# The last graph layer of a four-layer graph network: two heads side by side in TensorE's columns

## The chip, the cores and the metric

The kernel runs on one core of a Trainium2 chip. The metric is the device time of one execution in microseconds (us); lower is better. The engines of the core are named as in the profile: PE is TensorE (PEld its weight loads), DVE is VectorE, ACT is ScalarE, POOL is GpSimd, and SP issues transfers.

## The reference

The network takes 3125 nodes of 256 values and 100,000 edges through four layers. Each layer adds a graph layer and a mixer to the nodes, and then a feed-forward part. The change lies in the graph layer of the last one, a graph attention with four heads of 64 values:

```python
xp = (x @ W).reshape(n, N_HEADS, HEAD_DIM)
a_src = jnp.einsum('nhc,hc->nh', xp, att_src)
a_dst = jnp.einsum('nhc,hc->nh', xp, att_dst)
e = jax.nn.leaky_relu(a_src[src] + a_dst[dst], NEG_SLOPE)
e_max = jax.ops.segment_max(e, dst, num_segments=n)
e_exp = jnp.exp(e - e_max[dst])
denom = jax.ops.segment_sum(e_exp, dst, num_segments=n)
alpha = e_exp / denom[dst]
out = jax.ops.segment_sum(alpha[:, :, None] * xp[src], dst, num_segments=n)
```

So every target node gets, in each head, a weighted mean of the values of its source nodes. The result goes through relu and is added to x, together with the mixer of that layer (`_L3_mix_ref`, a linear attention with two layer norms and a small two-layer net). The last feed-forward part (one expert of eight per node) comes after both.

## The kernel before

**Layout.** Nodes stand in 25 blocks of 125 (`P = 125`, `NB = 25`). Targets are walked in pieces of 500 columns (`PW = 500`, `PIECES`: six of 500 and one of 125), two pieces at a time, so there are three groups of 1000 targets and a last one of 125.

**The dense form.** Nothing is gathered in this layer. An earlier stage has counted, for each pair of a source and a target, the edges between them and a loop per node, in bfloat16 (`ctt_d`). The weight of a pair is exp of a leaky relu of a sum, and this is the larger of two products of a source factor and a target factor. A factor that only the target has cancels in the division, so with r = exp(0.8 a_dst + bias), u0 = exp(a_src - top) and u1 = exp(0.2 (a_src - top)), the weight is max(r u0, u1). It is made for 125 sources and 1000 targets of a head in two instructions: ACT computes t = relu(r u0 - u1) (line 1899), DVE computes z = (t + u1) x counts (line 1902).

**Aggregation.** TensorE then multiplies z by the source values (line 1905). The stationary operand is `xr[:, b, k4, :]`, 125 sources by 65 columns: the 64 values of the head and a column of ones, which gives the sum of the weights. The moving operand is z, 500 targets at a time, and everything is float32. The result of a head and a piece, 65 x 500, adds up over the 25 source blocks in one PSUM bank; two heads and two pieces take the four banks `acc0` to `acc3`. In the loops, a group of targets (`p0`) holds two pairs of heads (`h0`), which hold 25 source blocks (`b`), which hold two heads (`h`) of two pieces (`k`). The last group takes all four heads at once, 125 targets of each. The counts of a block come through the SP queue into `cs`, which has three buffers, in two transfers, of 112 and of 13 rows (`move`, lines 134 and 135).

**Target factors.** At the start of each group, r is needed for all heads and targets, the same on all 125 partitions. Lines 1875 to 1881 make it on TensorE: the column of weights that gives a_dst is repeated 125 times as stationary operand and multiplied by the transposed nodes, two matmuls for each head and piece (line 1878), and ACT takes exp of the result (line 1880).

**End of a pair of heads.** The four banks are copied to SBUF by DVE and ACT in turn (`evac`, lines 141 and 143), TensorE turns them block by block (line 1920), and `finish` divides by the sum of weights, takes relu and adds to x, with five small DVE instructions for each block and pair of heads (lines 1860 to 1867). A sum below 1e-20 is noted in `few`; a note there would send the program into another, general path at the end.

**The order of work.** `l3_gnn_mix` runs the dense part and the mixer `l3_mix_by_pieces` together: `together` always advances the one whose reported progress is less, with the mixer's counted down by 1.15. All engines work down one fixed list, which the tile framework sets when the program is built. When both have finished a piece of nodes, `arrive` sends that piece on to the norm and the routing of the last feed-forward part.

Of the kernel before, what the change touches and what calls it, by code (L numbers as in the profile page):

```python
# [12 lines left out]
F32 = mybir.dt.float32  # L13
# [4 lines left out]
AF = mybir.ActivationFunctionType  # L18
OP = mybir.AluOpType
# [4 lines left out]
N = 3125  # L24
D = 256
P = 125
NB = 25
HB = D // 128
# [9 lines left out]
PW = 500  # L38
# [47 lines left out]
PIECES = [(i, min(PW, N - i)) for i in range(0, N, PW)]  # L86


class Net:
# [1692 lines left out]
    def l3_gnn_mix(self, before, arrivals):  # L1782
# [5 lines left out]
        nc, a = self.nc, self.a  # L1788
        with ExitStack() as s:
            ms = s.enter_context(self.pool("m3_sb"))  # L1790
            with self.pool("m3_w") as sb:
                w = self.load_w(sb, "L3_gnn_W")
                wx = self.attn_cols(sb, w, "wx", ["L3_gnn_att_src", "L3_gnn_att_dst"], ms)
            mix = self.l3_mix_by_pieces(ms, None)
# [4 lines left out]
            sb = s.enter_context(self.pool("g3_sb"))  # L1799
            wk = s.enter_context(self.pool("g3_wk", 2))  # L1800
            pa = s.enter_context(self.pool("g3_ps", 1, space=PSUM))
            xr = sb.tile([P, NB, 4, 65], F32, name="xr")
            nc.gpsimd.memset(xr[:, :, :, 64:65], 1.0)
            al = sb.tile([P, NB, 8], F32, name="al")
            for b in range(NB):
                ps = self.bank()
                self.mm_tok(ps[:P, :264], self.xt, b, wx)
                nc.vector.tensor_copy(xr[:, b, :, :64], ps[:P, :D].rearrange("p (h d) -> p h d", h=4))
# [9 lines left out]
            ps = self.bank()  # L1818
# [4 lines left out]
            bias = sb.tile([P, 4], F32, name="bias3")  # L1823
# [14 lines left out]
            self.together([self.l3_dense(sb, wk, pa, wx, xr, us, bias), mix], (1.0, 1.15))  # L1838

    def together(self, parts, pace=(1.0, 1.0)):  # L1840

# [5 lines left out]
            except StopIteration:  # L1847
                del at[p]

    def l3_dense(self, sb, wk, pa, wx, xr, us, bias):  # L1850
# [5 lines left out]
        at = free[:65, 8 * PW:12 * PW].rearrange("p (h d) -> p h d", h=2)  # L1856

        def finish(b, h0, nh, acc):

            nc.vector.tensor_scalar(few[:, b, h0:h0 + nh], acc[:, :, 64], 1e-20, None, op0=OP.is_lt)  # L1860
            rd = wk.tile([P, 4], F32, name="rd")
            nc.vector.tensor_scalar(rd[:, :nh], acc[:, :, 64], 1e-20, None, op0=OP.max)
            nc.vector.reciprocal(rd[:, :nh], rd[:, :nh])
            t = wk.tile([P, 4, 64], F32, name="tf")
            nc.vector.tensor_mul(t[:, :nh], acc[:, :, :64], rd[:, :nh, None].to_broadcast([P, nh, 64]))
            v = self.x[:, b, h0 * 64:(h0 + nh) * 64]
            nc.vector.scalar_tensor_tensor(v, t[:, :nh].rearrange("p h d -> p (h d)"), 0.0, v,
                                           op0=OP.max, op1=OP.add)

        done, there = 0, []  # L1870
        for p0 in range(0, len(PIECES), 2):
            pcs = PIECES[p0:p0 + 2]
            n = sum(w for _, w in pcs)
            for h in range(4):
                for k, (i, w) in enumerate(pcs):
                    ps = self.bank()
                    for c in range(HB):
                        nc.tensor.matmul(ps[:P, :w], wx[:, c, 260 + h:261 + h].to_broadcast([128, P]),
                                         self.xt[:, c, i:i + w], start=(c == 0), stop=(c == HB - 1))
                    nc.scalar.activation(rows[:, h, k * PW:k * PW + w], ps[:P, :w], AF.Exp, bias=bias[:, h:h + 1],  # L1880
                                         scale=0.8)
            hg = 4 if n < PW else 2
            for h0 in range(0, 4, hg):
                acc = {}
                for h in range(hg):
                    for k in range(len(pcs)):
                        acc[h, k] = pa.tile([65, 512], F32, name=f"acc{h * len(pcs) + k}")
                for b in range(NB):
                    cs = wk.tile([P, 2, PW], BF, name="cs", bufs=3)
                    if len(pcs) == 2:  # L1890
                        self.move(nc.sync, cs, self.ctt_d[p0:p0 + 2, :, b, :].rearrange("k p d -> p k d"))
                        c = cs.rearrange("p k d -> p (k d)")
                    else:
                        self.move(nc.sync, cs[:, 0, :n], self.ctt_d[p0, :, b, :n])
                        c = cs[:, 0, :n]
                    for h in range(hg):
                        k4 = h0 + h
                        t = wk.tile([P, 2 * PW], F32, name="t5")
                        nc.scalar.activation(t[:, :n], rows[:, k4, :n], AF.Relu, bias=us[:, 2, b, k4:k4 + 1],  # L1899
                                             scale=us[:, 0, b, k4:k4 + 1])  # L1900
                        z = wk.tile([P, 2 * PW], F32, name="z", bufs=3)
                        nc.vector.scalar_tensor_tensor(z[:, :n], t[:, :n], us[:, 1, b, k4:k4 + 1], c,  # L1902
                                                       op0=OP.add, op1=OP.mult)
                        for k, (i, w) in enumerate(pcs):
                            nc.tensor.matmul(acc[h, k][:, :w], xr[:, b, k4, :], z[:, k * PW:k * PW + w],  # L1905
                                             start=(b == 0), stop=(b == NB - 1))
                        done += n
# [5 lines left out]
                if hg == 2:  # L1913
                    for h in range(2):
                        for k, (i, w) in enumerate(pcs):
                            self.evac(at[:, h, k * PW:k * PW + w], acc[h, k][:, :w])
                    for j in range(n // P):
                        ps = self.bank()
                        for h in range(2):
                            nc.tensor.transpose(ps[:P, h * 65:(h + 1) * 65], at[:, h, j * P:(j + 1) * P],  # L1920
                                                self.ident[:65, :65])
                        finish(p0 * 4 + j, h0, 2, ps[:P, :130].rearrange("p (h c) -> p h c", h=2))
                        yield done / (NB * N * 4)
                else:
                    for h in range(4):
                        self.evac(at[:, h // 2, h % 2 * P:(h % 2 + 1) * P], acc[h, 0][:, :P])
                    ps = self.bank()
                    for h in range(4):
                        nc.tensor.transpose(ps[:P, h * 65:(h + 1) * 65], at[:, h // 2, h % 2 * P:(h % 2 + 1) * P],
                                            self.ident[:65, :65])  # L1930
                    finish(p0 * 4, 0, 4, ps[:P, :260].rearrange("p (h c) -> p h c", h=4))
# [426 lines left out]
```

## Time and profile before

| what | value |
|---|---|
| time, median of 7 runs | 4972.23 us (4964.39 to 4976.81) |
| profiled execution | 4981.08 us, span 4979.2 us |
| mean granted clock of TensorE over the span | 0.842 |
| dense stage of the last graph layer | 3801 to 4709 us, 908 us |
| TensorE, DVE, ACT busy in it | 878.4, 604.8, 534.5 us |
| aggregation (line 1905) | 1400 records, first at 3809.9, last at 4708.1 us |

A matmul of float32 stands in the trace as two records, each with its own weight load. A record's time on PE overlaps that of the next one, so the distance between starts tells what one costs. In a group of instructions, "128\*125 128x500" means 128 rows and 125 columns of stationary operand, and a moving operand of 500 columns.

### The profile page before, as it was taken

The numbers are of one execution on the slowest core, as the hardware profiler recorded it, in microseconds if no ns is written. First come the engines' busy times: TensorE is split into PE (matmuls) and PEld (weight loads), VectorE is DVE, ScalarE is ACT, GpSimd is POOL, SyncE is SP. The second block draws the span as 40 slices with busy tenths as digits, with TensorE's granted clock in tenths as the row PEclk, the third lists the DMA queues.
The fourth block names the chain that finished last, engine by engine and source line by source line (L and its number), as shares of the span: only waits on it lengthen the run. The fifth ranks groups of instructions, "written<-read, shape, count | busy, mean of one in ns | idle before, by whom it ended". The sixth has DMA issues, their size and how long they took to land. (4 is left out here: it accounts for less than half of the span.)

```text
span 4979.2 us, 49604 instructions
## 1 busy us (share of the span) xinstructions
PE 3795.7 (76%) x16425; PEld 2469.0 (50%) x16425; DVE 2466.1 (50%) x7872; ACT 1322.6 (27%) x2364; POOL 1125.2 (23%) x1124
## 2 busy tenths in 40 slices
PE   1886995899477799995555555455499999999798
PEld 0675993566345465554343333334265444444465
DVE  6885344544656311144343434445345666667644
ACT  1475100111132233331000000000045655455611
POOL 1000004000440100004666666666000000000011
PEclk8785995899787799997767677767699999999799
DMA  6244512433230000003333333333301112111142
GB/s 177 61 138 122 127 33 54 135 115 119 72 71 5 24 13 13 13 6 89 92 92 95 89 95 93 88 83 91 123 1 29 49 47 59 39 50 49 40 135 68
DMA packets 256291, 360.32 MB, mean 72 GB/s; under 512 B 62959, under 2 KB 199097, under 8 KB 256028
## 3 DMA queue, kind: packets, MB, share of 16 engines
q1 hardware_dynamic: 132514, 168.96, 11.7%
q0 software_dynamic: 66480, 135.56, 10.1%
q10 hardware_dynamic: 57033, 52.54, 3.8%
q8 instruction: 135, 2.21, 0.2%
q14 instruction: 129, 1.05, 0.1%
HBM read 270.31 MB, written 94.92 MB: 73 GB/s over the span
## 5 line engine op out<-in xcount | busy, mean ns | idle before, releaser
L1564 PE MATMUL acc<-hg,to 128*125 128x256 f32 x1682 | 584.5, 497 | 559.2 <-DVE to L1562 193.6
L1551 POOL DMA_INDIRECT hg<-hx_d,idx x841 | 827.4, 984 | 434.8 <-issue 241.4
L1564 PEld LDWEIGHTS acc<-hg,to 128*125 128x125 f32 x1682 | 382.3, 243 | 748.0 <-DVE to L1562 234.0
L1905 PE MATMUL acc<-z,xr 125*65 125x500 f32 (+1 forms) x1400 | 576.1, 554 | 10.4 <-DVE z L1902 8.5
L1902 DVE SCALAR_TENSOR_TENSOR z<-t,us,cs 125x1000 f32<-125x1000 f32 (+1 forms) x400 | 410.1, 1029 | 139.8 <-PE acc L1905 103.7
L1899 ACT ACTIVATE t<-xn,us 125x1000 f32<-125x1000 f32 (+1 forms) x400 | 409.6, 1037 | 237.4 <-DVE z L1902 232.3
L1905 PEld LDWEIGHTS acc<-z,xr 125*65 125x65 f32 x1400 | 188.4, 144 | 314.2 <-issue 272.5
L1562 DVE SCALAR_TENSOR_TENSOR to<-lock,keep,to 128x125 f32<-128x125 f32 x841 | 258.2, 345 | 169.0 <-remote 82.8
L1560 DVE TENSOR_SCALAR to<-iota_f,rel_b,wgt 128x125 f32<-128x125 f32 x841 | 269.2, 359 | 75.7 <-remote 46.2
L1422 DVE SCALAR_TENSOR_TENSOR x<-ps,lg,x 125x256 f32<-125x256 f32 x200 | 94.1, 483 | 415.4 <-PE ps L233 415.4
L239 PE MATMUL ps<-xt,w 128*128 128x500 f32 (+1 forms) x672 | 267.7, 545 | 1.8 <-DMA w<-in_L_ffn_W_dram 1.8
L2188 POOL DMA_INDIRECT bx_d<-row,slot x25 | 31.4, 1256 | 929.9 <-ACT t L1899 812.1
L779 ACT ACTIVATE k<-k 125x128 f32<-125x128 f32 x50 | 15.8, 317 | 801.5 <-DVE to L1562 322.5
L571 PE MATMUL ps<-y,cb 125*125 125x256 bf16 x1875 | 215.8, 280 | 0.0
L571 PEld LDWEIGHTS <-cb 125*125 125x125 bf16 x1875 | 214.5, 141 | 0.2
L168 ACT ACTIVATE rstd_t<-rstd_t 125x4 f32<-125x4 f32 (+2 forms) x86 | 17.3, 204 | 663.0 <-DVE rstd_t L167 420.1
L233 PE MATMUL ps<-wo,h 128*125 128x256 f32 x800 | 187.7, 386 | 3.6 <-ACT h L1416 2.6
L239 PE MATMUL ps<-h,w 128*128 128x500 f32 (+1 forms) x448 | 180.7, 546 | 7.8 <-ACT h L1411 7.8
L239 PEld LDWEIGHTS ps<-xt,w 128*128 128x128 f32 x672 | 122.4, 192 | 113.7 <-issue 108.1
L239 PE MATMUL pl<-xbt,w 128*128 128x384 f32 x416 | 172.2, 563 | 8.2 <-DVE xbt L1135 5.8
L233 PEld LDWEIGHTS ps<-wo,h 128*125 128x125 f32 x800 | 142.9, 187 | 65.8 <-ACT h L1416 43.7
L452 PE MATMUL t<-ky,lo 128*128 128x75 bf16 (+4 forms) x1251 | 138.7, 253 | 37.5 <-ACT ct L455 22.3
(558 smaller groups left out, 6179.4 us busy)
## 6 DMA issues: line engine op xcount, KB each, us to landing
cs<-ctt_d SPq DMA_DIRECT2D x150, 218.8 KB
w<-in_L_ffn_w_dram SPq DMA_DIRECT2D x52, 512.0 KB
cnt_d<-cd SPq DMA_DIRECT2D x25, 683.6 KB
cb<-cnt_d SPq DMA_DIRECT2D x25, 683.6 KB
ctt_d<-ct ACTq DMA_DIRECT2D x6, 2734.4 KB
hg<-hx_d,idx POOLq DMA_INDIRECT x841
b0x_d<-zero SPq DMA_DIRECT2D x1, 9984.0 KB
xb<-b0x_d SPq DMA_DIRECT2D x26, 384.0 KB
```

Source lines behind the costliest of these rows:

```text
L233: self.nc.tensor.matmul(ps, xt[:, h, b * P:(b + 1) * P], w[:, h, :], start=(h == 0), stop=(h == k - 1))
L239: self.nc.tensor.matmul(ps, w[:, h, :], xt[:, h, i:i + n], start=(h == 0), stop=(h == k - 1))
L452: nc.tensor.matmul(t[:, w * 25 * r:(w + 1) * 25 * r], lo[:, :, n % 4], ky[:, :25 * r, n % 4], start=(j == 0), stop=(j == ws[w0 + w][2] - 1))
L571: nc.tensor.matmul(ps[:P, :D], cf[k][:, h * P:(h + 1) * P], y3[:, b0 + k, j, :], start=(k == 0 and j == 0), stop=(k == m - 1 and j == 2))
L1422: nc.vector.scalar_tensor_tensor(self.x[:, b, :], ps[:P, :D], g[:, b, e:e + 1], self.x[:, b, :], op0=OP.mult, op1=OP.add)
L1551: nc.gpsimd.indirect_dma_start(out=hg[:, j, :], out_offset=None, in_=hx, in_offset=bass.IndirectOffsetOnAxis(ap=idx[:, c + j:c + j + 1], a ...
L1560: nc.vector.tensor_scalar(to, self.iota_f[:, :P], rel[:, c + j:c + j + 1], wgt[:, c + j:c + j + 1], op0=OP.is_equal, op1=OP.mult)
L1562: nc.vector.scalar_tensor_tensor(to, lock[:, b, :], keep[:, j:j + 1], to, op0=OP.max, op1=OP.mult)
L1564: nc.tensor.matmul(ps, to, hg[:, j, :D], start=(c + j == c0[b]), stop=(c + j == c0[b + 1] - 1))
L1899: nc.scalar.activation(t[:, :n], rows[:, k4, :n], AF.Relu, bias=us[:, 2, b, k4:k4 + 1], scale=us[:, 0, b, k4:k4 + 1])
L1902: nc.vector.scalar_tensor_tensor(z[:, :n], t[:, :n], us[:, 1, b, k4:k4 + 1], c, op0=OP.add, op1=OP.mult)
L1905: nc.tensor.matmul(acc[h, k][:, :w], xr[:, b, k4, :], z[:, k * PW:k * PW + w], start=(b == 0), stop=(b == NB - 1))
```

## The change

The heads of a pair share the columns of TensorE. The value matmul has 64 stationary columns instead of 65; the first head of the pair goes to columns 0 to 63, the second to 64 to 127 (`tile_position=(0, 64 * j)`), and both write one bank of 128 rows. The sums of weights are separate matmuls: 32 columns of ones, in tiles at columns 0, 32, 64 and 96 of a third bank, one for each head and piece. A half group uses three banks, and they rotate over four (`turn`).

The target factors are computed once for all nodes, before the loop: exp of `al` on ACT, one transpose on TensorE, a copy by DVE, a store to DRAM (`r_d`). `target_rows` loads them spread over the 125 partitions, through the SP queue, one load of 4 KB per partition for each head and group (again in parts of 112 and 13 rows), at the end of the half group that used those rows last.

`finish` copies three banks instead of four, turns the sums in one bank and the values in another for four blocks at once, and uses wider DVE instructions. The t tiles lie in a spare part of `xn`, z has four buffers instead of three, and TensorE's instructions of a block come after the z of all its heads.

```diff
-            xr = sb.tile([P, NB, 4, 65], F32, name="xr")
-            nc.gpsimd.memset(xr[:, :, :, 64:65], 1.0)
+            xr = sb.tile([P, NB, 4, 64], F32, name="xr")
...
+            r = sb.tile([P, 4, NB], F32, name="r3")
+            for h in range(4):
+                nc.scalar.activation(r[:, h], al[:, :, 4 + h], AF.Exp, bias=bias[:, h:h + 1], scale=0.8)
+            ps = self.bank()
+            nc.tensor.transpose(ps[:4 * NB, :P], r.rearrange("p h b -> p (h b)"), self.ident[:P, :P])
+            rt = sb.tile([4 * NB, P], F32, name="rt3")
+            nc.vector.tensor_copy(rt, ps[:4 * NB, :P])
+            r_d = self.dram.tile([4, N], F32, name="r3_d")
+            nc.sync.dma_start(r_d.rearrange("h (b p) -> (h b) p", p=P), rt)
...
+        def target_rows(g, h0):
+
+            if g < len(groups):
+                i, n = groups[g][0][0], sum(w for _, w in groups[g])
+                for h in (h0, h0 + 1):
+                    self.move(nc.sync, rows[:P, h, :n], r_d[h, i:i + n].partition_broadcast(P))
+
+        def finish(b, nb, h0, nh, acc):
+
+            w, nu = nb * P, len(acc) - 1
+            at = wk.tile([128, 3, PW], F32, name="at", bufs=1)
+            for k in range(nu + 1):
+                self.evac(at[:, k, :w], acc[k][:, :w])
+            ps = self.bank()
+            for j in range(nb):
+                nc.tensor.transpose(ps[:P, j * 128:(j + 1) * 128], at[:, nu, j * P:(j + 1) * P], self.ident)
...
-            for h in range(4):
-                for k, (i, w) in enumerate(pcs):
-                    ps = self.bank()
-                    for c in range(HB):
-                        nc.tensor.matmul(ps[:P, :w], wx[:, c, 260 + h:261 + h].to_broadcast([128, P]),
-                                         self.xt[:, c, i:i + w], start=(c == 0), stop=(c == HB - 1))
-                    nc.scalar.activation(rows[:, h, k * PW:k * PW + w], ps[:P, :w], AF.Exp, bias=bias[:, h:h + 1],
-                                         scale=0.8)
...
+            for hs in ((0, 2),) if len(pcs) == 1 else ((0,), (2,)):
+                units = [(h0, k, w) for h0 in hs for k, (_, w) in enumerate(pcs)]
+                acc = [pa.tile([128, 512], F32, name=f"acc{(turn + j) % 4}") for j in range(3)]
+                turn += 3
...
-                        for k, (i, w) in enumerate(pcs):
-                            nc.tensor.matmul(acc[h, k][:, :w], xr[:, b, k4, :], z[:, k * PW:k * PW + w],
-                                             start=(b == 0), stop=(b == NB - 1))
...
+                    for u, (h0, k, w) in enumerate(units):
+                        for j in range(2):
+                            nc.tensor.matmul(acc[u][64 * j:64 * j + 64, :w], xr[:, b, h0 + j, :],
+                                             zs[h0 + j][:, k * PW:k * PW + w], start=(b == 0), stop=(b == NB - 1),
+                                             tile_position=(0, 64 * j))
+                    for u, (h0, k, w) in enumerate(units):
+                        for j in range(2):
+                            q = 32 * (2 * u + j)
+                            nc.tensor.matmul(acc[2][q:q + 32, :w], self.ones[:P, :32],
+                                             zs[h0 + j][:, k * PW:k * PW + w], start=(b == 0), stop=(b == NB - 1),
+                                             tile_position=(0, q))
...
+                for h0 in hs:
+                    target_rows(g + 1, h0)
+                finish(b0, pcs[0][1] // P, hs[0], 2 * len(hs), acc)
```

More of the change, by code (lines that the diff above doesn't have):

```diff
@@ L1807, in l3_gnn_mix @@
                 self.mm_tok(ps[:P, :264], self.xt, b, wx)
-                nc.vector.tensor_copy(xr[:, b, :, :64], ps[:P, :D].rearrange("p (h d) -> p h d", h=4))
+                nc.vector.tensor_copy(xr[:, b], ps[:P, :D].rearrange("p (h d) -> p h d", h=4))
                 nc.scalar.copy(al[:, b, :], ps[:P, 256:264])
@@ L1837, in l3_gnn_mix @@
             mix.send(mw)
-            self.together([self.l3_dense(sb, wk, pa, wx, xr, us, bias), mix], (1.0, 1.15))
+            self.together([self.l3_dense(sb, wk, pa, xr, us, r_d), mix], (1.0, 1.15))
     def together(self, parts, pace=(1.0, 1.0)):
@@ L1848, in together, with l3_dense @@
                 del at[p]
-    def l3_dense(self, sb, wk, pa, wx, xr, us, bias):
+    def l3_dense(self, sb, wk, pa, xr, us, r_d):
         nc = self.nc
@@ L1855, in l3_dense @@
         rows = free[:, :8 * PW].rearrange("p (h d) -> p h d", h=4)
[L1856 to L1868, printed above, removed]
@@ L1870, in l3_dense @@
-        done, there = 0, []
-        for p0 in range(0, len(PIECES), 2):
-            pcs = PIECES[p0:p0 + 2]
-            n = sum(w for _, w in pcs)
-            for h in range(4):
-                for k, (i, w) in enumerate(pcs):
-                    ps = self.bank()
-                    for c in range(HB):
-                        nc.tensor.matmul(ps[:P, :w], wx[:, c, 260 + h:261 + h].to_broadcast([128, P]),
-                                         self.xt[:, c, i:i + w], start=(c == 0), stop=(c == HB - 1))
-                    nc.scalar.activation(rows[:, h, k * PW:k * PW + w], ps[:P, :w], AF.Exp, bias=bias[:, h:h + 1],
-                                         scale=0.8)
[L1882 to L1887, printed above, removed]
+        spare = [free[:P, j * PW:(j + 2) * PW] for j in (8, 10)]
@@ new lines, in l3_dense @@
+        groups = [PIECES[p:p + 2] for p in range(0, len(PIECES), 2)]
+        def target_rows(g, h0):
[11 more added lines that the diff above has]
+                nc.tensor.transpose(ps[:P, j * 128:(j + 1) * 128], at[:, nu, j * P:(j + 1) * P], self.ident)
+            sums = ps[:P, :nb * 128].rearrange("p (j q r) -> p j q r", j=nb, r=32)[:, :, :, 0]
+            rd = wk.tile([P, 4, 4], F32, name="rd")
+            f = wk.tile([P, 4, 4], F32, name="fw")
+            nc.vector.tensor_scalar(f[:, :nb], sums, 1e-20, None, op0=OP.is_lt)
+            nc.vector.tensor_scalar(rd[:, :nb], sums, 1e-20, None, op0=OP.max)
+            nc.vector.reciprocal(rd[:, :nb], rd[:, :nb])
+            for k in range(nu):
+                bk, hk = (b + 4 * k, h0) if nh == 2 else (b, 2 * k)
+                nc.vector.tensor_copy(few[:, bk:bk + nb, hk:hk + 2], f[:, :nb, 2 * k:2 * k + 2])
+                ps = self.bank()
+                for j in range(nb):
+                    nc.tensor.transpose(ps[:P, j * 128:(j + 1) * 128], at[:, k, j * P:(j + 1) * P], self.ident)
+                t = wk.tile([P, 4, 2, 64], F32, name="tf")
+                nc.vector.tensor_mul(t[:, :nb], ps[:P, :nb * 128].rearrange("p (j h d) -> p j h d", j=nb, d=64),
+                                     rd[:, :nb, 2 * k:2 * k + 2, None].to_broadcast([P, nb, 2, 64]))
+                v = self.x[:, bk:bk + nb, hk * 64:hk * 64 + 128]
+                nc.vector.scalar_tensor_tensor(v, t[:, :nb].rearrange("p j h d -> p j (h d)"), 0.0, v,
+                                               op0=OP.max, op1=OP.add)
@@ L1888, in l3_dense @@
+        done, there, turn = 0, [], 0
+        for h0 in (0, 2):
+            target_rows(0, h0)
+        for g, pcs in enumerate(groups):
+            b0 = pcs[0][0] // P
+            n = sum(w for _, w in pcs)
+            for hs in ((0, 2),) if len(pcs) == 1 else ((0,), (2,)):
+                units = [(h0, k, w) for h0 in hs for k, (_, w) in enumerate(pcs)]
+                acc = [pa.tile([128, 512], F32, name=f"acc{(turn + j) % 4}") for j in range(3)]
+                turn += 3
                 for b in range(NB):
@@ L1890, in l3_dense @@
                     if len(pcs) == 2:
-                        self.move(nc.sync, cs, self.ctt_d[p0:p0 + 2, :, b, :].rearrange("k p d -> p k d"))
+                        self.move(nc.sync, cs, self.ctt_d[2 * g:2 * g + 2, :, b, :].rearrange("k p d -> p k d"))
                         c = cs.rearrange("p k d -> p (k d)")
                     else:
-                        self.move(nc.sync, cs[:, 0, :n], self.ctt_d[p0, :, b, :n])
+                        self.move(nc.sync, cs[:, 0, :n], self.ctt_d[2 * g, :, b, :n])
@@ L1895, in l3_dense @@
                         c = cs[:, 0, :n]
[L1896 to L1902, printed above, removed]
-                                                       op0=OP.add, op1=OP.mult)
-                        for k, (i, w) in enumerate(pcs):
-                            nc.tensor.matmul(acc[h, k][:, :w], xr[:, b, k4, :], z[:, k * PW:k * PW + w],
-                                             start=(b == 0), stop=(b == NB - 1))
-                        done += n
+                    zs = {}
@@ new lines, in l3_dense @@
+                    for h in [h0 + j for h0 in hs for j in range(2)]:
+                        t = spare[h % 2]
+                        nc.scalar.activation(t[:, :n], rows[:P, h, :n], AF.Relu, bias=us[:, 2, b, h:h + 1],
+                                             scale=us[:, 0, b, h:h + 1])
+                        z = zs[h] = wk.tile([P, 2 * PW], F32, name="z", bufs=4)
+                        nc.vector.scalar_tensor_tensor(z[:, :n], t[:, :n], us[:, 1, b, h:h + 1], c,
+                                                       op0=OP.add, op1=OP.mult)
@@ L1908, in l3_dense @@
+                    done += n * 2 * len(hs)
                     yield done / (NB * N * 4)
@@ L1912, in l3_dense @@
                         there = []
[L1913 to L1931, printed above, removed]
+                for h0 in hs:
+                    target_rows(g + 1, h0)
+                finish(b0, pcs[0][1] // P, hs[0], 2 * len(hs), acc)
+                yield done / (NB * N * 4)
             there = [i for i, w in pcs]
```

## The prediction

> **What bounds the kernel now.** I read the page's engine rows first, then the table by stretches of time over the stage that the change touches, then the groups of instructions by shape inside it, and last single stretches of the timeline.
>
> ```profile
> PE 3795.7 (76%) x16425; PEld 2469.0 (50%) x16425; DVE 2466.1 (50%) x7872; ACT 1322.6 (27%) x2364; POOL 1125.2 (23%) x1124
> ...
> 3801.00:3960.00 159.00, 158.86 (x451) 65.29 (x450) 93.44 (x126) 99.64 (x136) 0.00 (x0) 1.00 0.18 49
> 3960.00:4110.00 150.00, 147.21 (x431) 64.52 (x430) 99.04 (x194) 86.41 (x97) 0.00 (x0) 0.99 0.17 47
> 4110.00:4260.00 150.00, 143.09 (x462) 67.70 (x462) 97.92 (x238) 79.16 (x85) 10.56 (x8) 0.99 0.19 51
> ...
> 4660.00:4709.00 49.00, 40.66 (x189) 26.92 (x188) 31.91 (x127) 34.96 (x81) 9.57 (x8) 0.71 0.09 15
> sum 908.00, PE 878.42 PEld 403.90 DVE 604.78 ACT 534.45 POOL 30.20; mean PE 125.49 PEld 57.70 DVE 86.40 ACT 76.35 POOL 4.32
> ```
>
> Columns of the stretches: from:to, length, busy time of PE, weight loads, DVE, ACT and POOL (instructions in brackets), granted clock, DMA share, GB/s. The dense stage of the last graph layer runs from 3801 to 4709 us. TensorE is busy 878.4 of 908 us, at a clock of 0.94 to 1.00 except in the last 49 us; DVE is busy 605, ACT 534. What changes in TensorE's work there changes the end, because the last feed-forward needs the finished nodes.
>
> ```profile
> L1905 PE MATMUL acc<-z,xr 125*65 125x500 f32 x1200 | 530.1, 585 | 2.8 <-DVE z L1902 2.8
> L1902 DVE SCALAR_TENSOR_TENSOR z<-t,us,cs 125x1000 f32<-125x1000 f32 x300 | 375.8, 1256 | 132.7 <-PE acc L1905 102.9 <-ACT t L1899 23.3 <-issue 2.3
> L1905 PE MATMUL acc<-z,xr 125*65 125x125 f32 x200 | 46.0, 366 | 7.6 <-DVE z L1902 5.7 <-issue 0.3
> L1878 PE MATMUL ps<-xt,wx 128*125 128x500 f32 x96 | 45.2, 633 | 0.3 <-DVE rd L1862 0.2
> ...
> 4001.07 0.14 PEld L1905 LDWEIGHTS acc<-z,xr 125*65 125x65 f32 x1 [0.28 <-issue]
> 4001.49 0.14 PEld L1905 LDWEIGHTS acc<-z,xr 125*65 125x65 f32 x1 [0.28 <-issue]
> ...
> 4035.45 3.52 PE L1905 MATMUL acc<-z,xr 125*65 125x500 f32 x8
> ...
> 796.02 1.54 PE L1058 MATMUL ps<-both,ones 125*128 125x400 f32 x2
> 797.36 0.68 PE L269 MATMUL ps<-ident,g 125*16 125x125 f32 x4
> ```
>
> In the groups the numbers after the bar are busy us, mean ns of one, and idle time before them with what ended it; in the timeline, start and duration in us. The program has 600 aggregation matmuls of 500 columns and the trace 1200 records: an f32 matmul is two passes, each with its own weight load. A pass occupies TensorE 0.42 us (eight take 3.52 with a tail of 0.58: 2.94/7); I use 0.419. The 585 ns of the group overlaps its neighbour and is no cost. And DVE waits 102.9 us on TensorE for a free z buffer, while TensorE waits 2.8 us on z: TensorE leads.
>
> **The change part by part.** The stage's tensor work before is 1200 x 0.419 = 503 us, 200 passes of 125 columns at about 0.107 = 21, the target factors (L1878) 96 x 0.419 = 40.2 plus 16 x 0.107 = 1.7, and 260 us of mixer and other work that stays.
>
> *Removed.* The target factors: 41.9 us of TensorE, nothing above it hides them. With them go 28 exponentials on ACT (24 take 15.9 us), off the path: ACT has 374 us to spare.
>
> *Matmuls.* A block (two heads, 1000 targets, 125 sources) had 4 matmuls, 8 passes, 3.35 us; there are 150. It now has 4 value matmuls in tiles of 64 columns and 4 sum matmuls in tiles of 32: 16 passes. No row of before shows two matmuls in TensorE at once, so I bound it. If tiles never run together: 16 passes, 1006 us. If they run together whenever their columns differ: 2 x 2 passes for the values and 2 for the sums, 6 per block, 377 us before losses. Between them stands what the trace does show: the 2750 passes and transposes of the stage start in the order of the program's list, and a matmul's second pass starts one pass after its first. If that order holds across tiles, the queue reads A-first, A-second, B-first, B-second: A-second must wait for A-first (same columns), B-first stands behind it. Starts are at 0, 1, 1, 2, then 2, 3, 3, 4: two overlap at most, however many tiles there are. Four sums so cost four passes, not two, and a block is 4 + 4 = 8 passes: no gain over before. I take this value, since it needs nothing but the order the rows show.
>
> It also has losses. When 128-column work (mixer, transposes) follows, it waits for the last second pass alone: one pass lost each time. I walked down the changed program's issue list with these rules. There, 500-column tile work is broken by 128-column work 126 times (53 us), and blocks are cut inside, where a sum needs columns a value pass still holds (47 us). Result: 604 us for the 500-column tiles and 32 for the last, 125-column group, against 503 + 21: +112. The other end is a change of tile size that waits until the array is empty: 64 to 32 columns and back is then 5 + 5 passes a block, and the list has 268 such changes in the 500-column part. The same walk gives 711 + 42: +229. The nearest row is the last pair shown, from 128 columns to a narrow tile: the 125x125 work starts 0.67 us after the last pass of 400 columns, the spacing which those two have themselves (1.54 less the tail of 0.87), so the change adds no extra time there; but with all columns taken it cannot say whether free columns may start early. I take the middle, +171.
>
> The Trainium skill, "TensorEngine Tiling (Array Packing)", Key Properties, says that a change of tiling mode drains TensorE, which speaks against this change; by it the sum would be the upper end, +229. The skill's "TensorE: Matmul & The Clock Gate", Part 3, reports 2.38 times for three column tiles, and also that matmuls are strictly FIFO in start and end; no run here shows either across tiles.
>
> *Finish.* Per half group: evacuations go from four of 65 rows to three of 128 (0.57 and 0.67 us each), transposes from 16 to 12, about 3 us less of TensorE in all. DVE's eight sets of five small operations (0.14 + 0.15 + 0.16 + 0.29 + 0.29 = 1.03 us) become three small ones and two wide pairs (about 0.7 each by the 65x500 row): 8.2 to 3.6 us, six times. DVE is not the bound; its cover, TensorE's passes, grows. The three rotating banks free the first bank early; I count zero, and if the cover is gone one evacuation (0.67) and one set (3.6) at seven ends, 30 us.
>
> *Target factors by DMA.* Four small exponentials, one transpose, a copy, a 50 KB write, then 32 spreading loads of 6.2 MB in all, on a stage with a DMA share of 0.17. At the start two transfers stand in series: by rows of the chain of waits, 2.75 us (a store of rows) and 8.64 (a load), 0 to 11 us, behind the mixer's first passes, which the list puts ahead: zero. On SP each later pair waits for ACT's last read of the rows and stands in front of half of the third block's counts; counts are three deep, so it costs zero, or at most a block (3.35 us) at six places, 20 us. Dropping the ones column moves nothing.
>
> *Waiting for both heads.* Value matmuls now need both z of a block where the first head could go ahead; z has four buffers instead of three and DVE makes two in 2.51 us, under the 3.35 of eight passes. Zero.
>
> *Sum.* +171 - 41.9 - 3 = +126. The profiled execution took 4981.1 us (span 4979.2 and 1.9 around it), 0.18% above the median 4972.2. 4981.1 + 126 = 5107; in the median's scale **5100 us**. This case's own range is +67 to +185, and up to +50 for the zeros: 5035 to 5190.
>
> **Rivals.**
>
> *Full overlap (other side).* If TensorE sends B-first while A-second still waits, pairs cost two passes and four sums cost two. The walk gives 426 + 22 us, or 466 + 42 if the array empties at each change of size, against 524: -76 or -16, and with the 44.9 removed -121 or -61. DVE does not stop it: 605 us of work in a stage of some 800. Time 4850 to 4912, middle 4881. It decides from the point where a block, losses included, costs under 8.7 passes (45 us are 0.7 of a pass a block). For it: separate columns can hold separate weights. Against: starts in program order.
>
> *No overlap (the change does not do what it says).* 1006 + 43 against 524, less 45: +480, 5450. For it: no overlap is in the trace. Against: the columns are disjoint by construction.
>
> *Boundaries and loads.* The zeros above all fail while passes stay at the low end: +67 + 50, 5090, within my case.
>
> **How the numbers follow.** In order: 0.53. Full overlap: 0.29. No overlap: 0.15, above my range. The rest, 0.03, is an even result, where full overlap's gain is eaten by losses. About 0.2%, 10 us, is what a measurement of this kernel tells from no change. Slower: 0.53 + 0.15 - 0.01 = 0.67; faster 0.30; same 0.03. The range 4872 to 5230 takes in the in-order case with weight loads partly uncovered (0.05 us on 1200 matmuls would be 60) and most of full overlap, and leaves out no overlap.
>
> **What would show it.** Right: within a block, B's first pass starts with A's second, not with A's first; 16 passes in 8 to 10 pass times; the target-factor rows gone; TensorE still over 90% busy from 3800 on and the stage some 975 to 1095 us long. Wrong to the fast side: two first passes starting within a few ns; four sums in two pass times. Wrong to the slow side: each pass 0.42 us after the one before, across tiles. Wrong elsewhere: TensorE idle at ends of halves on the spreading loads or on DVE.

## The result, and the profile after

| | before | changed |
|---|---|---|
| time, median | 4966.95 us (36 runs) | 5013.89 us (15 runs) |
| ratio to before | 1 | 1.0089, 95% interval 1.0072 to 1.0105 |
| profiled execution, span | 4979.2 us | 5018.9 us |
| granted clock over the span | 0.842 | 0.838 |
| first to last matmul of the groups of 500 columns | 823.5 us | 822.6 us |
| last group, of 125 columns | 74.7 us | 128.5 us |

The change makes the kernel 0.9% slower, some 45 us. Three of the 15 runs took only 4972 to 4979 us, at a mean clock of 0.844 to 0.847, the others 5010 us and more, at 0.831 to 0.839; no trace of one of the three was kept, so why they lose so little stays open. A second comparison, on another chip (run `e5_after_again` below), gave 1.0124, and its interval does not meet the first one. So an interval here holds for its own set of runs, and ratios of different chips are compared with some 0.3% of doubt.

The stage again, by stretches of time, before and then after. Columns: from:to, length, busy time of PE, weight loads, DVE, ACT and POOL with instructions in brackets, granted clock, DMA share, GB/s.

```profile
3810.00:4633.00 823.00, 807.18 (x2427) 356.59 (x2426) 547.98 (x1053) 472.36 (x535) 20.64 (x16) 0.99 0.18 49
4633.00:4708.00 75.00, 61.55 (x292) 42.86 (x290) 52.74 (x239) 53.92 (x120) 9.57 (x8) 0.70 0.12 26
```

```profile
PE 3857.4 (77%) x17689; PEld 2421.5 (48%) x17689; DVE 2433.1 (48%) x7688; ACT 1296.5 (26%) x2330; POOL 1129.3 (23%) x1123
...
3789.00:4612.00 823.00, 813.40 (x3523) 291.06 (x3522) 520.77 (x897) 454.61 (x512) 21.46 (x16) 0.99 0.20 55
4612.00:4740.00 128.00, 125.64 (x470) 58.11 (x466) 49.54 (x204) 50.95 (x110) 9.73 (x8) 0.53 0.07 15
```

The reader sees two things. The groups of 500 columns take 823 us in both kernels, although the target factors are gone from the second. The last group goes from 75 to 128 us, with TensorE busy throughout, at a clock of 0.53 where it had 0.70. That last group is the whole loss. From the end of the preparation of the values to the last aggregation matmul the stage is 49.4 us longer: 53.8 in the last group, -0.9 in the groups of 500 columns, -3.5 at the start. The rest of the 39.7 us in the span (+7.5 after the stage, -17.2 ahead of it) I can't assign: ahead of it nothing differs but the preparation, and single executions on one chip end that part 8 to 12 us apart.

The groups that answer to the aggregation of before (same stage, by shape: busy us, mean ns of one, idle before):

```profile
L1933 PE MATMUL acc<-z,xr 125*64 125x500 f32 x1200 | 358.9, 601 | 5.2 <-DVE z L1929 5.2
L1939 PE MATMUL acc<-z,ones 125*32 125x500 f32 x1200 | 201.4, 596 | 0.0
L1933 PE MATMUL acc<-z,xr 125*64 125x125 f32 x200 | 64.7, 429 | 1.9 <-DVE z L1929 1.9
...
L1929 DVE SCALAR_TENSOR_TENSOR z<-xn,us,cs 125x1000 f32<-125x1000 f32 x299 | 368.9, 1253 | 142.9 <-PE acc L1939 65.6 <-issue 36.9 <-ACT xn L1926 33.5
```

2400 passes of 500 columns now take 560.3 us of busy time, where 1200 took 530.1: they do run side by side. TensorE waits 5.2 us for z, DVE 65.6 us for TensorE, so TensorE is still the engine that leads. No wait on the spreading loads of the target factors shows on TensorE.

How a block runs is seen in the timeline of the changed kernel (start us, duration us). First a block between other blocks, then one that the mixer's work cuts:

```profile
4007.35 1.90 PE L1933 MATMUL acc<-z,xr 125*64 125x500 f32 x8
4009.18 1.04 PE L1939 MATMUL acc<-z,ones 125*32 125x500 f32 x8
4010.15 0.69 PE L1998 MATMUL ps<-xt,L_mix_W 128*128 128x500 f32 x1
...
3824.01 1.90 PE L1933 MATMUL acc<-z,xr 125*64 125x500 f32 x8
3825.84 1.02 PE L1939 MATMUL acc<-z,ones 125*32 125x500 f32 x2
3826.79 0.71 PE L1273 MATMUL ps<-va,k_e 125*128 125x129 f32 x4
3827.43 1.04 PE L1939 MATMUL acc<-z,ones 125*32 125x500 f32 x6
3828.40 0.69 PE L233 MATMUL ps<-wkv,xt 128*125 128x512 f32 x1
```

From its first start to the first start of what follows, the group of eight value passes takes 1.83 us and that of eight sum passes 0.98. In pass times of 0.419 us that is four and two, with 0.15 and 0.14 us over. The starts of the first block's records, in us, show the order:

```
value passes, 64 columns   4007.350 4007.357 | 4007.820 4007.827 | 4008.239 4008.246 | 4008.659 4008.665
sum passes, 32 columns     4009.178 .184 .191 .198 | 4009.621 .628 .634 .641
next, 128 columns          4010.154
```

Passes of different columns start 6 to 7 ns apart, and a tile's next pass starts 0.42 to 0.47 us after its last one. In the program's list the first head's matmul, of two passes, stands ahead of the second head's. Here the second head's first pass starts ahead of the first head's second one. This is the overlap in full.

This block alone leaves open whether the passes come to TensorE in that order already. Another one settles it. In the block that starts at 4056.860 us, the list has both matmuls of the first head ahead of both of the second head, and the first passes of both heads wait for their z. Counted from that start and told apart by their spacing, the first head's four passes start at 0, 0.470, 0.889 and 1.308 us, the second head's at 0.224, 0.694, 1.113 and 1.533. So the second head's first pass starts ahead of the first head's whole second matmul, which stands before it in the list. In the block at 4387.219, with the same list, the second head starts only at 1.519, after all four. So TensorE does not hold to the list's order across tiles: the second head's place among the first head's passes is not fixed by it.

The same starts show the price. Matmuls that run side by side are called a wave here; a wave is two passes long. Within one tile size, the passes of a tile are 0.419 us apart. The step into another size is 0.513 us (4008.665 to 4009.178, 4009.641 to 4010.154). From the first pass in the new size to the tile's next one it is 0.470 for 64 columns and 0.443 for 32: the weight load for a first pass starts with it, at nearly all changes of size in the stage 1 to 3 ns ahead of the pass, and so has no earlier pass to hide behind. For 128 columns and 512 moving ones that step is 0.531 in place of 0.429 (at 3822.1 us). Over the groups of 500 columns, 394 aggregation passes are followed by another size; 387 of these steps lie between 500 and 540 ns, with a mean of 513. After a mixer pass of 512 columns the step into another size is 0.522 in place of 0.429. And the cut block shows the second loss: one sum matmul runs alone, two passes and a change of size in 0.95 us, then comes a little mixer work, and then the three others need about the same time once more (0.97).

TensorE's list in the changed kernel has 520 changes of tile size in the groups of 500 columns and 208 in the last group; before there is none. It has 395 unbroken stretches of one size, which need 556 waves of two passes, where uncut blocks would need 150 x 3 = 450.

From this the aggregation of the 500-column groups can be added up. Blocks uncut and changes free: 450 x 0.838 = 377 us. Cuts: 106 x 0.838 = 89. Changes that follow an aggregation pass: 394 x 0.094 = 37. Uncovered loads: 201 changes into 64 columns at 0.05 and 193 into 32 at up to 0.025, some 14. The sum is 517. Measured, from each start to the next one: 535.9, against 518.0 before. Of the 19 us between count and measurement, 8 lie in the 11 stretches whose tiles start out of step; waits for z are 5 in all. The other 126 changes follow mixer passes and transposes, and those rows together rise by 12.6 us. The target factors save 31.3 (64 of their 96 passes of 500 columns lie in this stretch): 17.9 + 12.6 - 31.3 = -0.8.

### The profile page after: what moved, and what is told of

Same layout as the page of the kernel before. It is cut to its first block, busy times and chain, and to the rows that moved or that the text cites. A ratio compares the mean times of both kernels' runs of the same rounds, so it can differ in the third digit from the quotient of the medians.

```text
span 5018.9 us, 51902 instructions
## 1 busy us (share of the span) xinstructions
PE 3857.4 (77%) x17689; PEld 2421.5 (48%) x17689; DVE 2433.1 (48%) x7688; ACT 1296.5 (26%) x2330; POOL 1129.3 (23%) x1123
## 5 line engine op out<-in xcount | busy, mean ns | idle before, releaser
L1929 DVE SCALAR_TENSOR_TENSOR z<-xn,us,cs 125x1000 f32<-125x1000 f32 (+1 forms) x400 | 404.5, 1027 | 192.7 <-PE acc L1939 106.2
L1926 ACT ACTIVATE xn<-xn,us 125x1000 f32<-125x1000 f32 (+1 forms) x400 | 409.9, 1038 | 283.2 <-DVE z L1929 271.8
L1933 PE MATMUL acc<-z,xr 125*64 125x500 f32 (+1 forms) x1400 | 423.6, 577 | 7.1 <-DVE z L1929 7.1
L1939 PE MATMUL acc<-z,ones 125*32 125x500 f32 (+1 forms) x1400 | 261.1, 569 | 0.0
L1933 PEld LDWEIGHTS acc<-z,xr 125*64 125x64 f32 x1400 | 118.5, 145 | 256.0 <-issue 178.3
```

What stands on the lines that cost most here:

```text
L1926: nc.scalar.activation(t[:, :n], rows[:P, h, :n], AF.Relu, bias=us[:, 2, b, h:h + 1], scale=us[:, 0, b, h:h + 1])
L1933: nc.tensor.matmul(acc[u][64 * j:64 * j + 64, :w], xr[:, b, h0 + j, :], zs[h0 + j][:, k * PW:k * PW + w], start=(b == 0), stop=(b == NB - ...
L1939: nc.tensor.matmul(acc[2][q:q + 32, :w], self.ones[:P, :32], zs[h0 + j][:, k * PW:k * PW + w], start=(b == 0), stop=(b == NB - 1), tile_po ...
```

## The experiments

Theory: tiles overlap fully, and the gain is eaten by changes of tile size: by their own time, and in the last group by a lower granted clock. Rivals: the loads of the target factors, the new finish or the wait for both heads cost the time; or the cuts in the list alone do it; or the clock falls in the last group for another reason. The first four runs share a chip (before: 4825.11 us), so do the next four (4827.71 us on another one), and the last two (4971.04 us).

### The last group as before

One matmul of 65 columns per head in the group of 125 targets, four banks, the old finish there. The rest is the changed kernel.

```diff
+                    if last:
+                        for h in range(4):
+                            nc.tensor.matmul(acc[h][:65, :n], xr[:, b, h, :], zs[h][:, :n], start=(b == 0),
+                                             stop=(b == NB - 1))
-                    for u, (h0, k, w) in enumerate(units):
+                    for u, (h0, k, w) in enumerate(() if last else units):
```

> The changed kernel, but its last group of 125 targets is aggregated as before (65 stationary columns, no tiles). Changes of tile size in the program's list fall from 729 to 521. Theory (each change of tile size costs TensorE about 0.1 us and an uncovered weight load, and in the last group the changes also let the granted clock fall to a half): the aggregation of the last group goes from 100 us back to about 66, the clock there back to about 0.7, and the time to about 4975 us, 35 to 45 less than the changed kernel. Rival (the loss lies in the spreading loads or in the wide finish): the time stays within 10 us of 5014.

Measured: 4827.54 us, ratio 1.0003 [0.9994, 1.0013]. The whole loss is gone: 42 us by the first ratio of the changed kernel, 58 by the second.

```profile
3655.00:4478.00 823.00, 813.50 (x3520) 291.01 (x3522) 520.82 (x898) 454.21 (x512) 20.39 (x16) 0.99 0.21 55
4478.00:4551.00 73.00, 57.24 (x276) 39.46 (x268) 48.28 (x205) 48.62 (x111) 9.54 (x8) 0.70 0.13 26
```

The first stretch is the same to 0.1 us of TensorE as in the changed kernel, and the last group is back to 73 us at 0.70. The loads and the wait for both heads are still there in the groups of 500 columns, so whatever they cost is part of the gain that is missing there, and not of the loss.

### Target factors by DMA alone

The kernel before, with its target factors spread by DMA as in the change.

```diff
+        def target_rows(p0, h0):
...
+                    self.move(nc.sync, rows[:P, h, :n], r_d[h, i:i + n].partition_broadcast(P))
-                        nc.tensor.matmul(ps[:P, :w], wx[:, c, 260 + h:261 + h].to_broadcast([128, P]),
-                                         self.xt[:, c, i:i + w], start=(c == 0), stop=(c == HB - 1))
```

> The kernel before with one part of the change alone: the target factors are computed once and spread by DMA; aggregation, banks and finish are as before, and no tiles are used. Theory (tile changes): 4967 - 45 = about 4922 us. Rival (loads or waits on them eat what the removed matmuls gave): at or above the kernel before, up to 5010.

Measured: 4798.19 us, ratio 0.9940 [0.9923, 0.9956], 27 us less. The theory gave 45, the rival no gain. The stage, from the end of the preparation on, is 880.7 us against 919.1 before (profiled on different chips), 38 us less, which is nearly the 41.9 us of TensorE that were removed. The tail after the stage is 3 us longer. Some 8 us between stage and time are left open.

### Tiles of 32 columns only

The values of a head in two tiles of 32 columns, so that values and sums have one tile size. 1800 matmuls in place of 1200, the same work.

```diff
-                            nc.tensor.matmul(acc[u][64 * j:64 * j + 64, :w], xr[:, b, h0 + j, :],
-                                             ..., tile_position=(0, 64 * j))
+                            for c0 in (0, 32):
+                                q = 64 * j + c0
+                                nc.tensor.matmul(acc[u][q:q + 32, :w], xr[:, b, h0 + j, c0:c0 + 32],
+                                                 ..., tile_position=(0, q))
```

> The changed kernel with each value matmul of 64 columns split into two of 32 columns, so that values and sums have one tile size; 700 more matmuls, and 282 changes of tile size instead of 729. Theory (a change of tile size costs 0.1 us and an uncovered weight load): 447 fewer changes at 0.12 to 0.15 us are 54 to 67 us, and the last group overlaps again: 4920 to 4950 us. Rival (what costs is the number of matmuls and weight loads): slower than 5014, by up to 700 x 2 x 0.1 = 140 us.

Measured: 4768.60 us, ratio 0.9884 [0.9867, 0.9901]. Half as many matmuls again, and the time is 2.0 to 2.4% below the changed kernel (by its two ratios) and 56 us below the kernel before, a little more than the 17 to 47 of the theory. In the list, 256 changes of size in place of 520 in the groups of 500 columns and 26 in place of 208 in the last group.

```profile
3819.66 0.58 PE L239 MATMUL ps<-xt,L_mix_Wq 128*128 128x500 f32 x1
3820.17 1.88 PE L1935 MATMUL acc<-z,xr 125*32 125x500 f32 x16
...
3651.00:4409.00 758.00, 744.97 (x4726) 300.58 (x4726) 519.92 (x897) 454.95 (x509) 21.61 (x16) 1.00 0.23 59
4409.00:4486.00 77.00, 61.22 (x668) 40.05 (x662) 48.17 (x204) 48.60 (x110) 9.53 (x8) 0.76 0.13 26
```

Sixteen passes in four pass times: four tiles overlap as two do. The 500-column part loses 65 us and the last group 51, where the clock is back at 0.76. By the count used above, its 491 waves and their changes would take some 425 us; measured are 473. Of the other 48 us, 38 lie in 22 of the 129 unbroken stretches, those whose tiles start out of step, part of a pass apart.

### The tiles alone, without the target factors by DMA

The changed kernel, with its target factors on TensorE as before.

```diff
-                    self.move(nc.sync, rows[:P, h, :n], r_d[h, i:i + n].partition_broadcast(P))
+                        nc.tensor.matmul(ps[:P, :w], wx[:, c, 260 + h:261 + h].to_broadcast([128, P]),
+                                         self.xt[:, c, i:i + w], start=(c == 0), stop=(c == HB - 1))
```

> The changed kernel with the target factors made on TensorE at the start of each group as before; tiles, rotating banks and wide finish stay. Theory: 42 to 45 us more than the changed kernel, about 5057 us. Rival (the loads are what costs): 5014 or less.

Measured: 4916.67 us, ratio 1.0191 [1.0174, 1.0208]. That is 1.0% above the changed kernel by its first ratio and 0.7% by its second, 33 to 49 us, around the 41.9 removed. The tiles, with the banks and the finish that go with them, therefore cost about 90 us, and the target factors hide half of that.

### The changed kernel on a second chip

> The changed kernel once more, as a yardstick on this chip for the three runs beside it. Expected: 0.7 to 1.1% above the kernel before, as measured first (ratio 1.0089). Its last group of 125 columns should again run at a low granted clock (0.53 was measured) and take about 128 us against about 66 before.

Measured: 4890.43 us, ratio 1.0124 [1.0107, 1.0141], a little above what was expected. The last group takes 128.6 us again, at a clock of 0.53.

### More changes of size, and a control for them

Kernel one adds to the 32-column kernel a matmul of 128 stationary columns and one moving column, whose result nobody reads, between the values and the sums of each block of the 500-column groups. The control is the same kernel with 32 stationary columns in the added matmul.

```diff
+        def wide(z):
+            nc.tensor.matmul(self.bank()[:, :1], self.ones[:P, :], z[:, :1], start=True, stop=True)
...
+                    if len(pcs) == 2:
+                        wide(zs[hs[0] + 1])
```

```diff
-            nc.tensor.matmul(self.bank()[:, :1], self.ones[:P, :], z[:, :1], start=True, stop=True)
+            nc.tensor.matmul(self.bank()[:32, :1], self.ones[:P, :32], z[:, :1], start=True, stop=True,
+                             tile_position=(0, 0))
```

> The kernel of e3_all_tiles_32 with one more matmul per source block in the groups of 500 columns: 128 weight columns, one moving column, into a spare bank that nobody reads, between the value matmuls and the sums. It adds 136 matmuls and takes the changes of tile size in the 500-column part from 256 to 528. Theory (each change costs about 0.09 us, and the first pass after it an uncovered weight load): the stage 55 to 65 us longer than in e3_all_tiles_32, 0.40 to 0.45 us per inserted matmul, so near the time of the kernel before. Rival (the change of size is free, and what the changed kernel loses comes from pairs that the list cuts apart; here the pairs stay whole): at most 18 us, 0.13 us per inserted matmul, its own weight load.

Measured: 4883.15 us, ratio 1.0115 [1.0098, 1.0132]. The stage is 114 us longer than in the 32-column kernel, about twice what the theory gave and six times the rival's bound. But the run changes more than the sizes: the list is also cut into more pieces (515 waves for 491), and TensorE stands idle for 33 us in this part in place of 13, with a clock of 0.65 to 0.85 beside those waits. So this run alone does not tell the causes apart; the control does.

> The kernel of e6_three_sizes with each inserted one-column matmul on a tile of 32 weight columns in place of 128. TensorE's list is in the same order and has the same 150 inserted matmuls (the 136 in the expectation of e6_three_sizes counted only those that add a change), but 280 changes of tile size in the 500-column part in place of 528. Theory (it is the change of size that costs, 0.25 to 0.40 us for each inserted matmul with the two drains and the uncovered loads): 40 to 60 us less than e6_three_sizes, ratio 0.999 to 1.003 to the kernel before. Rival (e6_three_sizes is slow because its list is cut into more pieces and TensorE waits at the ends of groups): at most 20 us less, ratio 1.007 to 1.0115.

Measured: 4973.45 us, ratio 1.0011 [0.9995, 1.0028], about 50 us less than the three-size kernel (1.04% of the time; the stage 915.9 against 965.5 us). The same list, the same number of matmuls, 280 changes in place of 528: the changes cost 0.20 us each, with the uncovered loads, the inserted passes' own time, and the 12 waves (515 for 503, some 10 us) that are lost where the wide matmul cuts work of one size apart. The rival allowed 20 us. The waits are not the difference: TensorE stands idle no less in the control, 38 of 829 us. The timelines show one block of each, three sizes first, the control second:

```profile
3822.89 1.03 PE L1939 MATMUL acc<-z,xr 125*32 125x500 f32 x2
3823.84 0.38 PE L1907 MATMUL ps<-z,ones 125*128 125x1 f32 x2
3824.16 1.04 PE L1947 MATMUL acc<-z,ones 125*32 125x500 f32 x8
3825.13 1.12 PE L233 MATMUL ps<-wkv,xt 128*125 128x512 f32 x2
```

```profile
3964.22 0.61 PE L1940 MATMUL acc<-z,xr 125*32 125x500 f32 x1
3964.23 0.19 PE L1907 MATMUL ps<-z,ones 125*32 125x1 f32 x1
3964.24 0.61 PE L1948 MATMUL acc<-z,ones 125*32 125x500 f32 x2
...
3966.02 1.98 PE L233 MATMUL ps<-wkv,xt 128*125 128x512 f32 x4
```

With three sizes, the inserted matmul starts 0.95 us after the value matmul, when both its passes are through, and the sums start 0.32 us after that. With one size, it and the first sums start within 20 ns of the value pass, all in columns of their own. To the next mixer pass it is 2.24 against 1.80 us. What is left of the control above the 32-column kernel, some 64 us of the stage, is in part shown: 12 more waves are some 10 us, and tiles that start out of step, in 71 of 141 stretches for 22 of 129, hold another 28. The rest, the waits among it, I took no further apart.

### Changes of size in the last group alone, and a control

Four such matmuls per source block, in the last group only: first with 128, then with 32 stationary columns.

```diff
+                        if len(pcs) == 1:
+                            wide(zs[h0 + 1])
```

> The kernel of e3_all_tiles_32 with four such one-column matmuls per source block, but only in the last group of 125 columns: 26 changes of tile size become 146 there, and the work that the group needs stays as it is. Theory (the changes themselves lower the granted clock in a group of short matmuls): the last group goes from 77 to 110-130 us at a clock of 0.53 to 0.60. Rival (the clock falls there for another reason, the changes cost their 0.09 us alone): 77 to 90 us with the clock near 0.75.

> The kernel of e7_sizes_in_last_group with each inserted one-column matmul on a tile of 32 weight columns: the same order and number, 14 changes of tile size in the last group in place of 146. Theory (the changes of size bring the granted clock down): the last group back to 77 to 95 us with the clock above 0.6, ratio 0.988 to 0.993. Rival (any short matmuls put between bring it down): 125 to 141 us at 0.50, ratio 0.998 to 1.002.

Measured: ratio 1.0020 [1.0010, 1.0030] with 128 columns, 0.9918 [0.9887, 0.9950] with 32. The last group in the 32-column kernel was shown above (77 us, clock 0.76); with 128 columns and with 32 inserted:

```profile
4416.00:4557.00 141.00, 122.82 (x867) 91.00 (x861) 52.80 (x205) 52.57 (x110) 9.54 (x8) 0.53 0.07 15
```

```profile
4549.00:4637.00 88.00, 59.45 (x865) 41.12 (x862) 50.95 (x204) 49.04 (x110) 9.60 (x8) 0.75 0.11 23
```

The same number of matmuls in the same order: 146 changes of size give 141 us at a clock of 0.53, 14 changes give 88 us at 0.75. The first is more than the 110 to 130 us that were expected, the second as expected. So it is the changes that hold the clock down in short matmuls, not the short matmuls between. By what path they do it the runs do not show.

### A version with fewer changes

Tiles of 32 columns in the groups of 500, the last group with 65 columns as before, and the mixer let in after every second block only.

```diff
-                    yield done / (NB * N * 4)
+                    if b % 2:
+                        yield done / (NB * N * 4)
```

> The kernel of e3_all_tiles_32 with the last group of 125 columns as in the kernel before (one matmul of 65 columns per head), and the other work let in only after every second source block: 232 changes of tile size in the 500-column part in place of 256, none in the last group. Theory (each change avoided saves about 0.1 us): 2 to 5 us less than e3_all_tiles_32, and another 4 to 10 us from the last group. Rival (what is left of the changes costs nothing that can be measured): the same time as e3_all_tiles_32 within 0.2%, ratio 0.988 to the kernel before.

Measured: 4758.28 us, ratio 0.9864 [0.9848, 0.9881], the lowest ratio here: 69 us below the kernel before and 2.6% below the changed one on the same chip. Against the 32-column kernel it is 0.2% less, on another chip and with intervals that overlap, so the times do not tell the two apart; its stage is 11 us shorter (7 in the 500-column groups, 4 in the last), within the theory's 6 to 15.

```profile
3650.00:4400.00 750.00, 733.76 (x4720) 300.25 (x4718) 520.07 (x896) 453.23 (x508) 20.14 (x16) 1.00 0.23 60
4400.00:4474.00 74.00, 58.08 (x279) 40.35 (x271) 48.33 (x205) 49.09 (x112) 9.53 (x8) 0.68 0.12 26
```

## Why the prediction was wrong, by its steps

The forecast was 5100 us, +126; measured are +44 to +62 (the two ratios). The sign is right, the mechanism is not, so the sign is luck. Its own marks of the fast side are there, two first passes within a few ns and four sums in two pass times, and yet the kernel is slower. What happened lies nearest to the case that got 0.03, full overlap with its gain eaten by losses. One bound is added up wrongly (+185 and 50 on 4972 give 5207, not 5190); nothing rests on it.

**"If that order holds across tiles": failed.** This was the step that made a block eight passes. A block is four value pass times and two sum pass times, six. The rows of before could not show it, because all their passes use the same columns, where the order of the list and the order of the columns are the same thing. "Starts in program order" was read out of rows in which nothing could have started otherwise. The rule of the Trainium skill that stood beside it ("TensorE: Matmul & The Clock Gate", Part 3, strictly FIFO in start) does not fit these runs: in the block at 4056.860 the second tile's first pass starts at 0.224 us, ahead of a matmul that stands before it in the list and starts at 0.889.

**"The change adds no extra time" (of tile size): failed.** It was read from one pair in which a narrow matmul followed a full one, where 0.67 us was also the spacing of the pair before. That pair is of another kind: the granted clock there is 0.50, its matmul is a transpose without a tile position, and its weight load starts 0.665 us ahead of its pass, beneath the full one, where in the changed kernel the load starts with the pass. Measured in the stage, a step into another size takes 513 ns in place of 419, and the first pass after it 24 to 102 ns more for its weight load. That is 37 + 14 us on the aggregation's rows and most of the 12.6 by which the mixer's rows rose, some 60 us in all. The Trainium skill ("TensorEngine Tiling (Array Packing)", Key Properties) says that a change of tiling mode drains TensorE. The 94 ns agree with that, and the three-size run and its control show that the changes cost time; that TensorE empties in them is the page's account, which the starts fit.

**The losses by cuts.** The walk's 466 us for the 500-column part, under the rival of full overlap with the array emptied at each change, had the waves right: 556 x 0.838. With the 51 us that the changes add on these rows it comes to 517, and 535.9 was measured. So the rival with the array emptied was the mechanism; the price of each change was missing from it. Its 4912 us fell short for this and for the next point.

**The last group: mis-sized.** The walk gave 32 to 42 us against 21 before. Start to start, the aggregation there went from 54.8 to 112.4 us. Already the 21 was wrong: a clock of 0.71 stood in the last row shown, and the passes were costed at full clock, although that row was quoted. At 0.70 they would be some 31 us, an estimate; the rest of the 54.8 is waits and wider steps between short passes that I did not take apart. The fall from 0.70 to 0.53 could not be read from before; the run with the changes added and its control show where it comes from.

**Target factors removed: right in the stage.** 41.9 us were forecast; alone they gave 38 in the stage and 27 in the time, and 33 to 49 in the time with the tiles.

**The zeros.** The loads cost TensorE nothing that shows, and the run with the last group alone put back keeps them and the wait for both heads and has no loss, though it does not show the gain of the target factors either. The finish is not measured by itself. The tail behind the stage, 271 us before, is 274 to 281 in the variants, including the one that has only the target factors moved, so a few us may lie there; what they are stays open.

**The other rivals.** No overlap (5450 us) is ruled out by the first block shown. Boundaries and loads do not appear in TensorE's waits: z ahead of the value matmuls is 7.1 us in all.

## What to carry to other kernels

Matmuls in different column tiles overlap in full, so count waves per stretch of one tile size, not matmuls; and a change of the size cost 0.12 to 0.20 us here each time, a quarter to a half of a pass of 500 columns. Among short passes the changes also held the clock down. One tile size for all that stands together paid here even with half as many matmuls again. Before costing short matmuls, read the granted clock of just their stretch, and ask what the change does to it.

## What was not expected of the hardware

- Float32 matmuls, two passes each, start out of the list's order across column tiles: first passes 6 to 7 ns apart, each tile's second pass 0.44 to 0.47 us after its first, with two tiles and with four; and a matmul whose operand is ready starts 0.665 us ahead of one of another tile that stands before it in the list.
- A step into another tile size, among 32, 64 and 128: 513 ns in place of 419 after a pass of 500 columns, 522 in place of 429 after one of 512; from the first pass to the tile's next one 470 ns (64 columns) and 443 (32) in place of 419, and 531 in place of 429 (128 columns of stationary operand, 512 moving).
- Changes of size among matmuls of 125 moving columns hold the granted clock at 0.50 to 0.53, for over 100 us, with TensorE busy in 125.6 of 128 us; with one size in the same place it is 0.75, with TensorE busy in 59.5 of 88. The Trainium skill ("TensorE: Matmul & The Clock Gate", Part 1) lets the clock follow how busy TensorE has been. Here the busier stretch has the lower clock. A record lasts longer at a lower clock, so its busy time is in part an effect of it, and the busy share did not tell which stretch would have the low clock.
